# A planned scan kernel: the plan is told of the eight DMA semaphores, and dt and dt u are stored by chunks

## The chip, the core and the metric

The kernel runs on one core of a Trainium2 chip. The core has engines that each work through their own list of instructions in order: PE (TensorE, matmuls), DVE (VectorE), ACT (ScalarE), POOL (GpSimd) and SP (SyncE). SP computes nothing here; it issues transfers between the chip's memory and the core's on-chip memory. ACT and POOL issue some transfers too. The metric is the device time of one execution in microseconds; less is better.

## What is computed

Two layers of a vision network on an input of 4 images with 384 channels of 32 x 32 points, all in f32. In each layer a state-space scan comes first and a feed-forward part after it:

```
x = x + conv0(ln_c(x));  t = tokens(x);  t = t + ffn0(ln_t(t));  x = from_tokens(t)
x = x + conv1(ln_c(x));  t = tokens(x);  t = t + moe1(ln_t(t));  x = from_tokens(t)
```

`conv0` scans each image in four directions (rows, columns and both backwards), `conv1` is a Mamba block with 768 inner channels. The heart of both is the same recurrence over the 1024 points, with 16 states for each channel:

```
def step(h, inp):
    dtt, ut, bt, ct = inp
    dA = jnp.exp(dtt[..., None] * A)
    h = h * dA + (dtt * ut)[..., None] * bt[:, :, None, :]
    y = jnp.einsum('bkdn,bkn->bkd', h, ct)
    return (h, y)
```

dt, B and C come from projections of the input (`x_proj`, `dt_proj`, with a softplus on dt). `moe1` sends each token to the two best of four experts (384 to 1536 to 384 channels) and adds their outputs by gate weights.

## The kernel before

**The scan.** It is cut into 48 passes. A pass is one half of an image (T = 512 points) in one direction, or one half with half of the inner channels, for 384 channels. A pass has three parts (chunks of 128 channels), a part has four steps (four of the 16 states at a time): 576 steps in all. In a step the 128 partitions hold 32 channels times four states, and four groups x = 0..3 of 32 channels are treated one after the other:

- ACT computes the four decays exp(A dt) into PSUM tiles `da` (L1784) from the tile `dts`.
- POOL computes dt u times B for all four groups into a tile `s` (L1778) from `dtus` and `bt`; there are four `s` tiles.
- DVE runs the four recurrences (L1793) and multiplies some of the results by C (L1842); POOL multiplies the others (L1858). How many of the four POOL takes is chosen step by step by the plan (`split`). In a first half, the last column is kept in `state` (L1808 on DVE, L1857 on POOL).
- PE sums over the states into `acc` (L1814), and DVE adds `acc` to the output after the fourth step (L666 to L672, L918).

**What a pass needs first.** Two passes form a quad, which shares one projection: SP loads its weights `wx` (and `dtw`) from `ask_quad0` (L651, L652), PE multiplies (L637), ACT copies the result to `xd` (L642) and issues the store of the B and C rows (L494). `prep_pass` makes dt and dt u (L529 to L568) in tiles of [128 partitions, 3 chunks, 512], and `spread_out` (L511 to L514) stores both to a tile `spread` in the chip's memory, laid out as [chunk, 32 channels, group, 512]. `spread_pass` then reads it part by part, each row going to four partitions (the four states): on SP's queue one load of 1 MB into one of two `dtus` tiles (L590), on ACT's queue two loads of 512 KB into the three half tiles `dts` (L596). A `dtus` tile comes free when POOL has done the part before the last; the second `dts` half of a part has about one step between the decay that frees its tile and the decay that needs it. The rows of B and C are loaded for each pass by SP into `bt` and `ct` (L1775).

**Beside the scan** run layer norms, the feed-forward part of layer 0 (`post0`), the input projections and convolutions of layer 1 (`prep1`), its output (`post1`) and the experts (weights `mw` loaded at L1355, matmuls L1420 and L1442). What is left of the experts after the last scan forms the tail.

**What sets the order.** A planner in the kernel's Python (`Plan`) writes the order of each engine's list by simulating them before the kernel is built. An operation has a cost, the keys that it waits for, and so a time at which it could start; `run` takes the one that starts first, by the rules in `choose`, and emits it. Side work is written as generators: `yield SP, land(192)` asks for SP and says when the transfer will have landed. `land(kb)` is 3.5 + kb/200 us; an issue keeps SP for 0.1 us in the plan, whatever it issues. Where the plan sees PE idle, `fill` emits small matmuls that keep PE busy (L1833). The plan fixes the order alone; on the chip the instructions wait for semaphores.

**The semaphores of transfers.** In the built program every transfer that SP or ACT issues adds to one of eight semaphores, taken in turn over both queues, and waits, before it is issued, until the earlier transfer on that semaphore has landed, the eighth before it (2268 of the 2432 transfers carry this wait; others wait for a later one). An issue of ACT's that waits holds up ACT's other work. The plan before knows nothing of this.

Of the kernel before, what the change touches and what calls it, by code (L numbers as in the profile page):

```python
# [133 lines left out]

class Lane:
# [18 lines left out]
    def ready(self):  # L154
        return max(self.want[2] if len(self.want) > 2 else self.end, self.floor) + SLACK[self.rank >= LOW][self.want[0]]
# [11 lines left out]
class Plan:  # L167
# [39 lines left out]
    def mains(self, e):  # L207

        out = []
        for k in range(len(self.streams.get(e, ()))):  # L210
            op = self.head(e, k)
            if op is not None and all(d in self.end for d in op.deps):
                t = max([self.end[d] + LAG for d in op.deps], default=0.0) + op.lag
                out.append((max(self.free[e], t), k, op))
        return out
# [18 lines left out]
    def run(self):  # L234
        while True:
# [22 lines left out]
            start, what, e = best  # L258
            self.stuck = max(self.stuck, start)
# [4 lines left out]
            if isinstance(what, Lane):  # L264
# [5 lines left out]
                what.go(what.end, start)  # L270
            else:
# [4 lines left out]
                op.emit()  # L276


@with_exitstack
def layers(ctx, tc, ins, out, const):  # L280
# [160 lines left out]

    def layernorm(src, dst, eps, sq=None, sq_at=0.0, centred=False, scaled=True):
# [41 lines left out]
    def wload(src):  # L484

        w = yield from wts.take()
        yield SP, land(192) + 2.5
        nc.sync.dma_start(out=w.rearrange("p c m -> p (c m)"), in_=src)
        return w

    def rows_out(q, to):

        q["rows"] = q.get("rows") or dram.tile([2 * NS, L], F32, tag="rows", name="rows", bufs=4)
        nc.scalar.dma_start(out=q["rows"][:, to], in_=xd[q["at"] : q["at"] + 2 * NS, to])  # L494
# [12 lines left out]
    def load_dtw(q, k):  # L507

        nc.sync.dma_start(out=dtw[dt_rows(q), :], in_=ins["w_dt1"][:, k * D : (k + 1) * D])

    def spread_out(to, of):  # L511

        for q in range(NG):
            nc.sync.dma_start(out=to[:, :, q, :].rearrange("c r t -> r c t"), in_=of[q * QP : (q + 1) * QP])  # L514
# [60 lines left out]
    def spread_pass(p):  # L575
# [3 lines left out]
        def gen():  # L579
            spread, stored = st.pop(("spread", p))  # L580
            for part in range(NC):
# [8 lines left out]
                nc.sync.dma_start(out=dtus[n % 2].rearrange("p q t -> p (q t)"), in_=of(1, 0, NG))  # L590
                plan.end["dtu", p, part] = plan.now + land(1024)
                for x in range(2):
                    m = 2 * n + x - 3
                    before = (yield from until(("da", 4 * (m // 2) + 3, 2 * (m % 2) + 1))) if m >= 0 else 0.0
                    yield ACT, 0.55, max(before, stored)
                    nc.scalar.dma_start(out=dts[(2 * n + x) % 3].rearrange("p q t -> p (q t)"), in_=of(0, 2 * x, 2))  # L596
# [5 lines left out]
    def prep0(b):  # L602
        u = st[("u0", b)]

        def ln(h):
            def gen():
                yield SP, land(768)
                nc.sync.dma_start(out=u[h], in_=half(x_in[b], h))
                yield from layernorm(u[h], u[h], eps6)
# [38 lines left out]
    def ask_quad0(q, k):  # L648
        def gen():
            yield SP, land(66)  # L650
            nc.sync.dma_start(out=wx0.rearrange("p c m -> p (c m)"), in_=ins["w_x0"][k])  # L651
            nc.sync.dma_start(out=dtw[dt_rows(q), :], in_=ins["w_dt0"][k])  # L652
# [21 lines left out]
    def post0(b, h):  # L674
# [15 lines left out]
        def add_x(c):  # L690
            def gen():
                xh = yield from t1.take()
                yield SP, land(256)
                nc.sync.dma_start(out=xh, in_=piece(x_in[b], c, h))
# [8 lines left out]
        def ln2():  # L703
# [8 lines left out]
            nc.sync.dma_start(out=fold[:, :, :32], in_=fold_d)  # L712
# [14 lines left out]
        def ffn(lane):  # L727
            def gen():
# [6 lines left out]
                for i in range(2 * lane, 2 * lane + 2):  # L735
                    w, proj1 = yield from wts.two()
                    yield SP, land(192) + 2.0
                    nc.sync.dma_start(
                        out=w.rearrange("p a m -> p (a m)")[zrow, :], in_=ins["w_fc1"][:, i * NC * P : (i + 1) * NC * P]
                    )  # L740
                    nc.sync.dma_start(
# [29 lines left out]
        def ffn_out():  # L771
# [4 lines left out]
            nc.sync.dma_start(out=spread.rearrange("p a m -> p (a m)"), in_=of)  # L776
# [12 lines left out]
            nc.sync.dma_start(out=half(x1[b], h), in_=y)  # L789
# [11 lines left out]
    def prep1(b, h):  # L801
# [6 lines left out]
        def conv(i):  # L808
            def gen():
                for j in range(NC):  # L810
# [8 lines left out]
                    nc.sync.dma_start(out=dg, in_=taps_d[c])  # L819
# [33 lines left out]
        def gate(i):  # L853
            def gen():
# [14 lines left out]
                nc.scalar.dma_start(out=to.rearrange("(c p) t -> p c t", p=P), in_=z)  # L869
# [16 lines left out]
    def prep_quad1(q, b, h):  # L886
        def gen():
# [3 lines left out]
            nc.sync.dma_start(out=wx1, in_=ins["w_x1"].rearrange("p (c m) -> p c m", c=NI))  # L891
# [28 lines left out]
    def post1(b, h, early=False):  # L920
# [3 lines left out]
        def gate(i):  # L924
            def gen():
# [3 lines left out]
                nc.sync.dma_start(out=z, in_=of.rearrange("(c p) t -> p c t", p=P))  # L929
# [14 lines left out]
        def project():  # L944
            o = st["o", b, h] = yield from tmp.take()
            for m in range(NC):
                w = yield from wts.two()
                yield SP, land(384)
                for i in range(2):
                    nc.sync.dma_start(out=w[i], in_=w_out[m, :, i * NC : (i + 1) * NC])  # L950
# [20 lines left out]
        def add_x(m):  # L971
            def gen():
# [3 lines left out]
                nc.sync.dma_start(out=xh, in_=piece(x1[b], m, h))  # L976
# [12 lines left out]
        def end():  # L989
            o = st["o", b, h]  # L990
            t = yield SP, STORE
            nc.sync.dma_start(out=x2[b, h].rearrange("(c p) t -> p c t", p=P), in_=o)
# [16 lines left out]
    def centre():  # L1009
# [9 lines left out]
        for c in range(NI):  # L1019
# [7 lines left out]
            nc.sync.dma_start(out=taps_d[c], in_=dg)  # L1027
            t1.give(dg)
        plan.end["taps",] = plan.now
        for i in range(2):  # L1030
# [4 lines left out]
            nc.sync.dma_start(out=w, in_=ins["w_out"][i * D : (i + 1) * D].rearrange("(c p) m -> p c m", p=P))  # L1035
# [8 lines left out]
            for m in range(NC):  # L1044
                nc.sync.dma_start(out=out_d[m, :, i * NC : (i + 1) * NC], in_=w[:, :, m * P : (m + 1) * P])
            tmp.give(t)

    def zero():
# [4 lines left out]
        for slot in (*slot_x, *slot_y):  # L1053
            for x in range(slot.shape[0] // P // n):
                to = slot.rearrange("(n p) d -> p n d", p=P)[:, n * x : n * (x + 1), :]
                yield SP, 12.0
                nc.sync.dma_start(out=to, in_=rep(z[:, :D], n))
# [265 lines left out]
    def experts():  # L1323
# [21 lines left out]
        def weights():  # L1345

            for s, i in every:
# [4 lines left out]
                for q in range(2 * NQ):  # L1352
                    w = yield from mws.take()
                    yield SP, 0.1
                    nc.sync.dma_start(out=w, in_=of[q])  # L1355
                    wq.append((plan.now + land(393) + 1.0, w))

        def fetch():

            for n, (s, i) in enumerate(every):  # L1360
# [11 lines left out]
                nc.sync.dma_start(  # L1372
# [3 lines left out]
                nc.sync.dma_start(  # L1376
# [115 lines left out]
        def keep():  # L1492

            for s0, _ in every:
# [16 lines left out]
                for k in range(m):  # L1511
                    yield SP, land(192)
                    nc.sync.dma_start(out=slot_y[g % 3][bass.DynSlice(at + k * P, P)], in_=rows[k][:, :D])
# [6 lines left out]
    def combine(u):  # L1520
# [4 lines left out]
        def begin():  # L1525
            x = st["out", u] = yield from tmp.take()
            yield SP, land(768)
            nc.sync.dma_start(out=x, in_=x2[u].rearrange("(c p) t -> p c t", p=P))

        def some(j):  # L1530
            def gen():
# [10 lines left out]
                nc.sync.dma_start(out=b2, in_=ins["b2"])  # L1542
# [30 lines left out]
        def end():  # L1573
# [3 lines left out]
            nc.sync.dma_start(out=to, in_=x)  # L1577
# [3 lines left out]
        def early():  # L1581
# [3 lines left out]
            nc.sync.dma_start(out=b2[:NE, :D], in_=ins["b2"])  # L1585
# [9 lines left out]
        def by_rows(j):  # L1595
            def gen():
# [32 lines left out]
                nc.sync.dma_start(out=to, in_=part)  # L1629
# [143 lines left out]
    def load(p, m, of, to):  # L1773
        rows = passes[p]["q"]["rows"][of + 4 * m : of + 4 * m + 4, cols(passes[p]["h"])]
        nc.sync.dma_start(out=to[m], in_=rows.unsqueeze(0).to_broadcast([QP, 4, T]))  # L1775
# [211 lines left out]

    plan = Plan(
# [10 lines left out]
def land(kb):  # L1999

    return 3.5 + kb / 200
# [105 lines left out]
```

## Time and profile before

| what | value |
|---|---|
| three runs | 5034.54, 5049.6, 5051.74 us (median 5049.6) |
| profiled execution | 5032.81 us, its span 5031.0 us, mean granted clock of PE 0.894 |
| busy over the span | PE 85%, DVE 83%, POOL 80%, ACT 60% |
| first and last scan of DVE | 99.4 us and 4472.7 us |
| transfers | 899.33 MB, 179 GB/s |

The page's second part shows the span in 40 slices (tenths of each engine's time):

```profile
PE   8777778887767799988877798899888888899999
DVE  4999999999999899999989999999999999850002
ACT  4544458765545577767654577767685756554442
POOL 2999999999988898989988988889899988850002
```

DVE and POOL are at nine tenths until the scan ends, some 35 slices in; PE takes over for the tail. The transfers of interest, from the page's last part (what, queue, count, size of one):

```profile
dts<-dts ACTq DMA_DIRECT2D x288, 512.0 KB
dtus<-dts SPq DMA_DIRECT2D x144, 1024.0 KB
dts<-tmp SPq DMA_DIRECT2D x376, 192.0 KB
```

The name `dts` stands for the half tiles, and also for the `spread` tile in the chip's memory: `dts<-dts` is a load from the one to the other, and `dts<-tmp` is a store of `spread_out` (eight more read from another pool, 384 in all). The time of a landing is not on the page; where one is given, it is the last update of the transfer's semaphore in the trace.

### The profile page before, as it was taken

What the parts mean: (1) busy time and instruction counts of PE and PEld (TensorE: products, weight loads), DVE (VectorE), ACT (ScalarE), POOL (GpSimd) and SP (SyncE); (2) the same over time, 40 slices, a digit from 0 to 9 for tenths busy, and PEclk for the clock granted to TensorE, in tenths of its full rate; (3) what the DMA queues carried; (4) which work ended last, traced back from release to release, by engine and by line L of the source; (5) the groups of instructions that cost most, each with busy time, mean ns of one, the idle gap of its engine ahead of it and who ended that gap; (6) DMA issues with size and microseconds to landing.
All of it is one profiled execution on the core that took longest, in us unless ns stands there. A gap on an engine that the chain in (4) does not pass through costs nothing. (4 is left out here: it accounts for less than half of the span.)

```text
span 5031.0 us, 57132 instructions
## 1 busy us (share of the span) xinstructions
PE 4262.9 (85%) x17967; PEld 2192.9 (44%) x17967; DVE 4159.0 (83%) x5754; ACT 3037.3 (60%) x4769; POOL 4006.4 (80%) x1826
## 2 busy tenths in 40 slices
PE   8777778887767799988877798899888888899999
PEld 3222222222223454444444454345534333569996
DVE  4999999999999899999989999999999999850002
ACT  4544458765545577767654577767685756554442
POOL 2999999999988898989988988889899988850002
PEclk9887889888888899999987899899988889899998
DMA  4344656654443565556564655466655454655556
GB/s 148 110 161 156 205 169 214 207 185 139 161 143 107 195 193 175 190 188 211 188 221 161 215 181 175 155 197 205 230 179 191 155 181 148 220 184 180 170 165 190
DMA packets 394191, 899.33 MB, mean 179 GB/s; under 512 B 62384, under 2 KB 143520, under 8 KB 375456
## 3 DMA queue, kind: packets, MB, share of 16 engines
q1 hardware_dynamic: 336672, 704.28, 43.3%
q10 hardware_dynamic: 49024, 166.22, 9.7%
q0 software_dynamic: 8192, 25.17, 1.6%
q8 instruction: 143, 2.34, 0.2%
q14 instruction: 160, 1.31, 0.1%
HBM read 712.11 MB, written 183.40 MB: 178 GB/s over the span
## 5 line engine op out<-in xcount | busy, mean ns | idle before, releaser
L1778 POOL TENSOR_TENSOR s<-dtus,bt 128x2048 f32<-128x2048 f32 x576 | 2605.3, 4533 | 178.1 <-PE acc L1814 67.2
L1784 ACT ACTIVATE da<-dts,a 128x512 f32<-128x512 f32 x2304 | 1530.2, 686 | 886.4 <-DVE s L1842 771.5
L1814 PE MATMUL acc<-s,four 128*32 128x512 f32 x4608 | 735.1, 682 | 382.0 <-POOL s L1858 344.9
L1858 POOL TENSOR_TENSOR s<-s,ct 128x512 f32<-128x512 f32 (+1 forms) x552 | 942.5, 1708 | 138.6 <-DVE s L1793 102.0
L1793 DVE TENSOR_TENSOR_SCAN da<-da,s 128x512 f32<-128x512 f32 x775 | 918.2, 1216 | 114.0 <-ACT da L1784 82.4
L1842 DVE TENSOR_TENSOR s<-da,ct 128x512 f32<-128x512 f32 x1529 | 1009.6, 680 | 0.1
L1793 DVE TENSOR_TENSOR_SCAN da<-da,state,s 128x512 f32<-128x512 f32 x754 | 939.5, 1277 | 17.7 <-ACT da L1784 10.1
L1833 PE MATMUL acc<-ident,few 128*32 128x256 f32 x2886 | 751.5, 416 | 36.2 <-DVE big L918 18.6
L1833 PEld LDWEIGHTS acc<-ident,few 128*32 128x32 f32 x2886 | 334.4, 119 | 510.6 <-issue 225.1
L1793 DVE TENSOR_TENSOR_SCAN s<-da,state,s 128x512 f32<-128x512 f32 x398 | 495.5, 1267 | 8.7 <-ACT da L1784 8.6
L1793 DVE TENSOR_TENSOR_SCAN s<-da,s 128x512 f32<-128x512 f32 x377 | 447.1, 1204 | 17.3 <-ACT da L1784 17.3
L1814 PEld LDWEIGHTS acc<-s,four 128*32 128x32 f32 x4608 | 106.5, 113 | 748.9 <-POOL s L1858 547.3
L1420 PE MATMUL ps<-tmp,mw 128*128 128x256 f32 (+1 forms) x1812 | 387.9, 369 | 22.3 <-ACT tmp L1465 11.5
L1442 PE MATMUL ps<-mw,tmp 128*128 128x192 f32 x2096 | 377.1, 337 | 17.5 <-DMA mw<-in_w_dram 6.8
L1442 PEld LDWEIGHTS ps<-mw,tmp 128*128 128x128 f32 x2096 | 350.4, 195 | 82.4 <-issue 42.9
L1420 PEld LDWEIGHTS ps<-tmp,mw 128*128 128x128 f32 x1812 | 316.5, 198 | 135.7 <-issue 30.4
L1615 DVE SCALAR_TENSOR_TENSOR big<-big,gk,da 128x384 f32<-128x384 f32 x2 | 1.2, 612 | 414.2 <-PE da L1613 414.2
L1605 POOL DMA_INDIRECT big<-ys,slot x12 | 11.8, 980 | 382.7 <-DMA ys<-t 379.3
L799 PE MATMUL ps<-big,w 128*128 128x512 f32 x576 | 280.2, 627 | 14.3 <-DMA w<-in_w_in_dram 8.2
L568 POOL TENSOR_TENSOR tmp<-tmp,big 128x256 f32<-128x256 f32 (+1 forms) x186 | 193.0, 1063 | 68.3 <-DVE tmp L1037 68.3
L529 PE MATMUL ps<-xd,dtw 12*128 12x512 f32 (+1 forms) x288 | 187.9, 743 | 17.2 <-ACT tmp L542 9.4
L838 PE MATMUL ps<-tmp,t 128*128 128x512 f32 x368 | 175.3, 620 | 15.6 <-ACT tmp L830 9.9
(448 smaller groups left out, 5322.2 us busy)
## 6 DMA issues: line engine op xcount, KB each, us to landing
mw<-in_w_dram SPq DMA_DIRECT2D x414, 384.0 KB
dts<-dts ACTq DMA_DIRECT2D x288, 512.0 KB
dtus<-dts SPq DMA_DIRECT2D x144, 1024.0 KB
dts<-tmp SPq DMA_DIRECT2D x376, 192.0 KB
bt<-rows SPq DMA_DIRECT2D x192, 256.0 KB
ct<-rows SPq DMA_DIRECT2D x192, 256.0 KB
dts<-in_w_dram SPq DMA_DIRECT2D x78, 384.0 KB
ys<-t SPq DMA_DIRECT2D x32, 768.0 KB
```

The lines of the kernel that those rows point to most:

```text
L529: nc.tensor.matmul(pd, lhsT=dtw[dt_rows(q), c * P : (c + 1) * P], rhs=xd[dt_rows(q), cols(h)], start=True, stop=True,)
L568: nc.gpsimd.tensor_tensor(to, by, u[:, c], ALU.mult)
L799: nc.tensor.matmul(pi, lhsT=w[:, c, :], rhs=u[:, c], start=c == 0, stop=c == NC - 1)
L1420: nc.tensor.matmul(ph[:, k * width : (k + 1) * width], lhsT=w[:, c, k * P : (k + 1) * P], rhs=turned[:, c], start=c == 0, stop=c == NC - 1,)
L1442: nc.tensor.matmul(py[:, k * HD : (k + 1) * HD], lhsT=by_f(hids[half_], width)[:, at_, k * P : (k + 1) * P], rhs=w[:, f], start=4 * q + f ...
L1778: nc.gpsimd.tensor_tensor(ss[i % NSR], dtus[part_of(i) % 2], rep(bts[i % 4], NG), ALU.mult)
L1784: nc.scalar.activation(das[x], dts[(2 * part_of(i) + x // 2) % 3][:, x % 2, :], AF.Exp, scale=v["a"][:, g, m : m + 1])
L1793: nc.vector.tensor_tensor_scan(d if in_psum else s, d, s, 0.0 if v["first"] else state[:, v["slot"], j, x : x + 1], ALU.mult, ALU.add)
L1814: nc.tensor.matmul(acc[x * QP : (x + 1) * QP, :], lhsT=four, rhs=ss[i % NSR][:, x, :], start=m == 0, stop=m == 3)
L1833: nc.tensor.matmul(acc[:QP, : 2 * P], lhsT=nil.to_broadcast([P, QP]), rhs=rep(ident, 2), start=fresh, stop=fresh)
L1842: nc.vector.tensor_tensor(ss[i % NSR][:, x, :], das[x], cts[i % 4], ALU.mult)
L1858: nc.gpsimd.tensor_tensor(s[:, m:, :], s[:, m:, :], rep(cts[i % 4], NG - m), ALU.mult)
```

## The change

It has two parts. First, the planner keeps a model of the eight semaphores (`Ring`): every transfer of SP and ACT goes through `ask`, which notes when the transfer could be issued, keeps the queue for 0.55 us, and computes a landing from a common rate of 220 KB/us. No transfer is planned before the eighth before it has landed by this model. `land` is changed with it. The times of tiles that are given back follow from these.

Second, `spread_out` stores one chunk per transfer (three of 256 KB, each from all 128 partitions) in place of one group of 32 channels per transfer (four of 192 KB, each from 32 partitions). What is stored, and where, is the same.

```diff
+class Ring:
+    at = busy = 0.0
+    lands = [0.0] * 8
+    n = 0
...
+    @classmethod
+    def next(cls):
+        return cls.lands[cls.n % 8] + 0.1
+
+    @classmethod
+    def issue(cls, kb):
+        t = max(cls.at, cls.next())
+        cls.busy = max(t + 1.2, cls.busy) + kb / RATE
+        cls.lands[cls.n % 8] = cls.busy + 1.0
+        cls.n += 1
+        cls.at = t + ISSUE
...
     def ready(self):
-        return max(self.want[2] if len(self.want) > 2 else self.end, self.floor) + SLACK[self.rank >= LOW][self.want[0]]
+        least = Ring.next() - LAG if self.want[0] == SP or len(self.want) > 3 else 0.0
+        return max(self.want[2] if len(self.want) > 2 else self.end, self.floor, least) + SLACK[self.rank >= LOW][self.want[0]]
...
                 t = max([self.end[d] + LAG for d in op.deps], default=0.0) + op.lag
-                out.append((max(self.free[e], t), k, op))
+                out.append((max(self.free[e], t, Ring.next() if e == SP else 0.0), k, op))
...
             start, what, e = best
+            Ring.at = start
...
                 what.go(what.end, start)
+                self.free[e] = max(self.free[e], Ring.at) if Ring.at > start else self.free[e]
...
                 op.emit()
+                if e == SP:
+                    self.free[e] = max(self.free[e], Ring.at)
...
+    def ask(queue, out, in_):
+        Ring.issue(int(np.prod(out.shape)) / 256)
+        queue.dma_start(out=out, in_=in_)
...
     def spread_out(to, of):
-        for q in range(NG):
-            nc.sync.dma_start(out=to[:, :, q, :].rearrange("c r t -> r c t"), in_=of[q * QP : (q + 1) * QP])
+        for c in range(NC):
+            ask(nc.sync, out=to[c].rearrange("r q t -> q r t"), in_=of[:, c])
...
-                    yield ACT, 0.55, max(before, stored)
-                    nc.scalar.dma_start(out=dts[(2 * n + x) % 3].rearrange("p q t -> p (q t)"), in_=of(0, 2 * x, 2))
+                    yield ACT, 0.55, max(before, stored), True
+                    ask(nc.scalar, out=dts[(2 * n + x) % 3].rearrange("p q t -> p (q t)"), in_=of(0, 2 * x, 2))
...
+    Ring.reset()
     plan = Plan(
...
 def land(kb):
-    return 3.5 + kb / 200
+    return 3.2 + kb / 220
+
+RATE, ISSUE = 220.0, 0.55
```

All other issues of SP and ACT inside the planned part are changed from `dma_start` to `ask` in the same way. Since the plan's times move, the whole order moves with them: the built program has 2336 transfers of SP and ACT instead of 2432, DVE's multiplications by C are 1514 instead of 1529, and the filling matmuls (L1833) are 1538 instead of 1443.

## The prediction

> **What bounds the kernel now.** I read the windows view first, cut at the first scan (99 us) and the last one (4474 us).
>
> ```profile
> core 0: us, PE busy (x) PEld busy (x) DVE busy (x) ACT busy (x) POOL busy (x), PEclk, DMA share, GB/s
> 99.00:4474.00 4375.00, 3624.02 (x14791) 1688.88 (x14791) 4082.64 (x5459) 2766.88 (x4312) 3949.51 (x1769) 0.88 0.54 179
> 4474.00:5031.00 557.00, 548.89 (x2891) 467.29 (x2889) 43.43 (x127) 224.26 (x381) 46.75 (x45) 0.96 0.58 178
> ```
>
> For 4375 us DVE is busy 93% and POOL 90%: the scan phase, 576 steps of 7.6 us, ends when DVE has done its work and its 292 us of idle time. After it PE is busy 99% with the experts that are left. In the built order of instructions the matmuls after the last scan sum (L1814) are the same in both kernels, 688 of L1442 and 540 of L1420 among them, so I cost the tail at nothing (at most its 8 us of idle PE could go); its weight loads would cost something only if they came later than now. All of the change must show in the scan phase.
>
> There I ask which of DVE's waits a transfer ends, in the view of all waits (total us, times, longest):
>
> ```profile
> ACT xd L642 <- PE ps L637: 106.8, 14, 15.7
> PE ps L637 <- DMA wx<-in_w_x_dram: 93.8, 12, 14.9
> DVE da L1793 <- ACT da L1784: 92.5, 39, 14.1
> POOL s L1778 <- DMA dtus<-dts: 39.8, 4, 19.9
> ACT da L1784 <- DMA dts<-dts: 35.0, 14, 6.5
> ```
>
> Read downwards the first three are one chain: the weights of a quad (wx) land late, PE's L637 waits, the copy L642 waits in ACT's queue, the decays L1784 wait behind that copy, and DVE runs dry. I followed each DVE gap over 1.5 us back through its releasers. Seven gaps end in this chain (4.8, 9.9, 5.9, 7.9, 14.1, 7.3 and 5.0: 55 us); four end in late dts or dtus loads (19 us); three in the store L789 (12 us). So 86 of DVE's 292 idle us are owed to transfers. The other gaps (among them 94 us behind PE's sums) have nothing to do with them.
>
> Why wx is late shows in SP's timeline at one such place (columns: start, length, what):
>
> ```profile
> 1657.84 3.68 SPq L514 DMA_DIRECT2D dts<-tmp  x4
> 1662.24 0.54 SPq L1775 DMA_DIRECT2D bt<-rows  x1
> 1662.89 0.58 SPq L1775 DMA_DIRECT2D ct<-rows  x1
> 1663.53 0.59 SPq L590 DMA_DIRECT2D dtus<-dts  x1
> 1664.21 8.83 SPq L514 DMA_DIRECT2D dts<-tmp  x4
> 1673.09 0.43 SPq L651 DMA_DIRECT2D wx<-in_w_x_dram  x1
> ```
>
> wx stands right behind the four stores of dt u. Those took 8.83 us to issue, because each waits for the transfer eight before it. PE waits for wx until 1675.4, ACT copies at 1680.9, and DVE's 14.1 us gap ends at 1683.6.
>
> **The change, part by part.**
>
> *The work.* By the built order, DVE's multiplications by C (L1842) go from 1529 to 1514 and its state copies (L1808) from 775 to 762: 15 x 0.680 + 13 x 0.147 = 12.1 us less. POOL takes them: 6 more double ones (2.355 us each), 3 more single (1.270), 5 more copies (0.19): 18.9 us. Cover for that: POOL's 425 idle us in the phase; without it, +18.9. Term: -12.
>
> *Stores by chunk.* 384 stores of 192 KB become 288 of 256 KB; bytes and 2 KB pieces stay the same. What moves is the outermost dimension of the DRAM side: 32 rows before, four groups of 32 channels now. The trace has one transfer with a four outermost, the load of spread_d (L776, 8 times, 192 KB). In the record of semaphore updates it shows five, the first after 1.0 us and four that come with the data; a store of the kernel before shows sixteen. It lands after 4.8 to 13.1 us, median 5.7; a 192 KB load over sixteen lands after 2.4 us when the queues are quiet. So a four outermost means four of the sixteen DMA engines. In that row the four stands on the source's side, in the new stores on the destination's. [...] If a four on the destination's side did nothing, the stores would run on sixteen as now, and the terms for wx and for the other transfers would fall to nothing: -22 in place of +73. I take four, as the row has it.
>
> A store is then 32 pieces on each of four engines; a 2,048-byte packet took 105 ns in the mean: 3.4 us, and 10.1 us for three stores. With the 2.5 us that a quiet spread load takes beyond its own 32 packets (4.8 less 32 x 0.071), the last lands 12.6 us after the first issue. The 96 groups of four in the trace had their last landing 6.1 us after the first issue (median). Difference: 6.5 us later. Readers of the stores don't notice: in both orders 44 of 48 passes store five to ten steps (38 us and more) before their first load. What is queued behind the stores notices.
>
> *wx, behind them.* In the new order wx still stands right behind a dt u store at 13 of 16 quads, so it comes 6.5 us later: 85 us over all. The new schedule answers with ACT's copy L642, which moves by one step later in all over those quads (five moves of 0.5 to 2.75 steps later, three of 0.75 to 3.25 earlier, the rest a quarter or none): 7.6 us of relief. Of PE's lateness DVE saw all at the seven quads that already stall (45 us) and, I take it, half at the other six (20). Term: +55. Bounds: -55 (the stalls vanish) and +85.
>
> *The other transfers.* Each pass (91 us) puts 192 pieces, 20.2 us, on each of the four engines, where it put 5.0 on each of sixteen. Of the 144 dts loads that have only a step to land in, 22% meet a store under way: 32. Each has 8 packets of 191 ns on an engine, 1.5 us, and sharing doubles it; fourteen already come late and the rest has hardly more room. Term: +25, bounds 0 and +109 (32 times one whole store, 3.4 us). ACT's own issues wait for the transfer eight before too; where that is a store (47 issues, as before) nine instead of seven come within a step of it. The decays are queued behind such an issue, and DVE waits for those. Term: +10, bounds 0 and 9 x 6.5 = 59. The dtus and bt loads follow the stores in SP's queue, but have four steps to land in: +5, bounds 0 and 40 (POOL's waits for dtus once over).
>
> *The schedule that knows.* Each issue now costs 0.55 us in the plan instead of 0.1, and none goes before the transfer eight back has landed. An issue took 0.33 to 0.59 us in the trace, so this is nearer the truth. But the plan lands a 256 KB store 3.4 us after its issue, and by the row above that is too early by 2 to 7 us. It can remove what is left of DVE's waits for transfers, 31 us; I take a third. Term: -10, bounds -31 and +25 (a reshuffled order with new small gaps). POOL's and PE's queues are reordered with it; no row prices that beyond this bound.
>
> Sum: -12 + 55 + 25 + 10 + 5 - 10 = +73 us. The profiled execution took 5032.8 us for its span of 5031.0, below all three runs (5034.5, 5049.6, 5051.7). The middle of the four is 5042, so I predict **5115 us**.
>
> **The rivals.**
>
> *The knowledge pays.* If stores that land 6.5 us later are hidden (eight steps of room), and the plan puts PE's L637 and ACT's copies where wx really lands, about half of the 86 us goes with the 12: 5042 - 55 = 4987; all of it, 4944. For it: the chain is caused by just what the plan did not know. Against it: wx still stands behind the same stores, at the same steps. It decides from the point where ACT's waits for L642 fall below some 50 us. Chance of faster: 0.22.
>
> *It does not do what it says.* The order around the quads hardly moves, and what the plan gains the stores give back: 5042 - 12 + 10 = 5040, within 5017 to 5067. Chance 0.14.
>
> *The ring closes.* The eight semaphores are held by slow stores, and ACT itself is held at its issues: half of 47 x 6.5 us on top of the sum gives 5270. Against it: at only nine of the 47 does the store stand close. Chance 0.05, part of the slower side.
>
> *The forecast*, slower: 0.59, its own range 5070 to 5185. A measurement of this kernel can tell 0.5%, 25 us, from no change. Faster by more than that 0.22, within 0.14, slower 0.64. The range reaches down into the first rival and up past the middle of the bounds: 4985 to 5185.
>
> **What would show it.** Stores L514 with five semaphore updates instead of sixteen and a last landing 12 us after the first issue: the engine count. "ACT xd L642 <- PE ps L637" growing from 107 to 150 us or more: the wx term; falling below 60: the first rival. "ACT da L1784 <- DMA dts<-dts" above 60: the shared engines. The last scan at about 4545 us and a tail of 557: that the tail stays out of it. Sixteen updates on the new stores would make the prediction wrong at its root.

## The result and the profile after

| | before | after |
|---|---|---|
| runs | 5034.54 to 5051.74 us, median 5049.6 (5) | 5199.88 to 5216.13 us, median 5207.18 (5) |
| profiled span | 5031.0 us | 5209.6 us, granted clock of PE 0.887 |
| start of DVE's first scan, end of its last | 99.4 and 4474 us | 103.7 and 4648 us |

The change makes the kernel 3.3% slower: ratio 1.033, 95% interval 1.0315 to 1.0344. In the medians that is 158 us, in the two profiled spans 179 us. The prediction said slower, and 5115 us; the time lies above its range.

The windows view of after, cut at the first and the last scan, answers to the one shown of before (columns: busy us and count of each engine, granted clock, DMA share, GB/s):

```profile
104.00:4648.00 4544.00, 3669.46 (x14971) 1721.77 (x14972) 4070.59 (x5431) 2765.03 (x4312) 3967.03 (x1783) 0.88 0.51 173
4648.00:5209.60 561.60, 552.94 (x2906) 469.53 (x2904) 43.43 (x126) 224.31 (x381) 46.32 (x45) 0.96 0.58 177
```

Of the 179 us, 169 lie in the scan phase (4544 against 4375). DVE's work there fell, by 12.0 us (4082.6 to 4070.6); its idle time rose from 292 to 473 us. The tail is 5 us longer (561.6 against 557.0), the start 4 us.

The waits view of after (total us, times, longest) shows the chain from before grown at every link:

```profile
DVE da L1829 <- ACT da L1820: 220.4, 78, 16.6
ACT xd L678 <- PE ps L673: 190.9, 14, 20.7
...
PE ps L673 <- DMA wx<-in_w_x_dram: 153.6, 12, 19.3
...
ACT da L1820 <- DMA dts<-dts: 35.2, 14, 6.2
...
POOL s L1814 <- DMA dtus<-dts: 26.4, 1, 26.4
ACT da L1820 <- DMA dts<-tmp: 26.4, 4, 8.8
```

(L1829, L1820, L678 and L673 are L1793, L1784, L642 and L637 of before; all issues are now at L476, in `ask`.) PE waits 154 us for wx instead of 94, ACT's copy 191 instead of 107, DVE 220 instead of 93. The waits for dts and dtus loads, on which another term of the prediction stood, have not grown. The last line is new. (An "..." in a fence marks lines that are not shown.)

One place in the timeline of after shows the whole chain (start, length, engine, what, idle time before and its releaser):

```profile
1317.24 2.11 SPq L476 DMA_DIRECT2D dts<-tmp  x3
1319.40 3.22 SPq L476 DMA_DIRECT2D dtus<-dts  x1
1322.66 1.09 SPq L476 DMA_DIRECT2D wx<-in_w_x_dram  x1
...
1334.07 5.35 PE L673 MATMUL ps<-big,wx 128*44 128x512 f32 x12 [15.94 <-DMA wx<-in_w_x_dram]
...
1339.47 0.58 ACT L678 COPY xd<-ps 44x512 f32<-44x512 f32 x1 [20.69 <-PE ps L673]
1339.95 0.69 ACT L1820 ACTIVATE da<-dts,a 128x512 f32<-128x512 f32 x1
...
1340.74 1.29 DVE L1829 TENSOR_TENSOR_SCAN da<-da,state,s 128x512 f32<-128x512 f32 x1 [16.25 <-ACT da L1820]
```

Three stores of dt u go out from 1317.2 on; wx is issued at 1322.7, and PE starts only at 1334.1, 11.4 us after that issue. ACT's copy follows, the decays stand behind it in ACT's queue, and DVE has been idle for 16 us when its scan starts at 1340.7.

How late the transfers land was read from the updates of their semaphores (medians; a landing is the last update, counted from the issue):

| transfer | before | after |
|---|---|---|
| updates of one store `dts<-tmp` | 16 | 5 |
| its landing | 3.85 us | 11.16 us |
| a set of stores, first issue to last landing | 6.1 us (four) | 15.1 us (three) |
| wx, behind the stores of dt u | 2.80 us | 11.19 us |
| ct loads, median and 90th percentile | 4.12, 7.0 us | 5.44, 11.4 us |
| w_in loads, the same | 3.74, 6.2 us | 4.34, 9.9 us |
| dts loads (ACT's queue) | 5.87 us | 6.16 us |

A new store shows its five updates at 0.95, 10.01, 10.04, 10.08 and 12.05 us (one store as an example): the first at once, four with the data.

The packets tell the same. Between the first issue and the last landing of a set of stores, 23 sets of before and three of after have no 2 KB packets on SP's queue but their own 384. In before 16 of them are in flight at once most often (31% of that time, never more than 20), in after four (62%, never more than six).

The updates of wx show what those stores do to it. Its load counts sixteen. In before the 12th comes after 2.60 us and the 16th after 2.80 (medians of 16 loads). In after the 12th comes after 3.39 us, and the last four follow late: the 16th after 11.19. At the 14 loads that are issued while stores are under way, the step of over 1 us between the 12th update and the 13th is there every time, and at 13 of the 14 the last update comes 0.2 to 0.3 us after the last of those stores has landed. So twelve parts of the load are as good as on time, and four, as many as the parts of a store, end when the stores do.

To size the terms, every gap of DVE over 0.2 us between the first and the last scan was followed back through its releasers to the transfer, or to the engine where the trail ends (us of DVE's idle time; smaller groups, 80 us before and 89 us after, are only in the last row):

| gap ends in | before | after |
|---|---|---|
| wx | 72 | 167 |
| a store (`dts<-tmp`) that has not landed | 0 | 34 |
| other loads on SP's queue: w_in, mw, expert rows `tmp<-xs`, fold, taps, ct | 31 | 70 |
| dts loads | 13 | 6 |
| dtus loads | 14 | 0 |
| the store L789 (`x<-big`) | 12 | 4 |
| ACT's decays, no transfer found | 57 | 90 |
| all | 279 | 460 |

### The profile page after: what moved, and what is told of

The parts are those of the page before. It is cut to its first block, busy times and chain, and to the rows that moved or that the text cites. A ratio compares the mean times of both kernels' runs of the same rounds, so it can differ in the third digit from the quotient of the medians.

```text
span 5209.6 us, 57475 instructions
## 1 busy us (share of the span) xinstructions
PE 4311.9 (83%) x18157; PEld 2227.7 (43%) x18157; DVE 4147.1 (80%) x5726; ACT 3035.6 (58%) x4769; POOL 4024.1 (77%) x1840
## 3 DMA queue, kind: packets, MB, share of 16 engines
q1 hardware_dynamic: 331680, 704.26, 40.8%
## 5 line engine op out<-in xcount | busy, mean ns | idle before, releaser
L1820 ACT ACTIVATE da<-dts,a 128x512 f32<-128x512 f32 x2304 | 1529.9, 686 | 854.0 <-DVE s L1878 692.2
L1894 POOL TENSOR_TENSOR s<-s,ct 128x512 f32<-128x512 f32 (+1 forms) x561 | 960.4, 1713 | 149.9 <-DVE s L1829 114.8
L1829 DVE TENSOR_TENSOR_SCAN da<-da,s 128x512 f32<-128x512 f32 x762 | 902.9, 1216 | 175.3 <-ACT da L1820 142.3
L1829 DVE TENSOR_TENSOR_SCAN da<-da,state,s 128x512 f32<-128x512 f32 x752 | 936.4, 1276 | 80.0 <-ACT da L1820 78.1
L1869 PE MATMUL acc<-ident,few 128*32 128x256 f32 x3076 | 784.1, 410 | 35.1 <-DVE big L954 13.9
L1869 PEld LDWEIGHTS acc<-ident,few 128*32 128x32 f32 x3076 | 352.4, 118 | 526.3 <-issue 227.8
L1829 DVE TENSOR_TENSOR_SCAN s<-da,state,s 128x512 f32<-128x512 f32 x400 | 498.0, 1266 | 30.2 <-ACT da L1820 30.2
L1829 DVE TENSOR_TENSOR_SCAN s<-da,s 128x512 f32<-128x512 f32 x390 | 462.4, 1205 | 24.3 <-ACT da L1820 24.1
L1456 PE MATMUL ps<-tmp,mw 128*128 128x256 f32 (+1 forms) x1752 | 366.2, 365 | 22.3 <-DMA mw<-in_w_dram 14.2
L1456 PEld LDWEIGHTS ps<-tmp,mw 128*128 128x128 f32 x1752 | 303.6, 197 | 123.7 <-issue 46.7
```

Of the source, the lines that this page charges most:

```text
L1456: nc.tensor.matmul(ph[:, k * width : (k + 1) * width], lhsT=w[:, c, k * P : (k + 1) * P], rhs=turned[:, c], start=c == 0, stop=c == NC - 1,)
L1820: nc.scalar.activation(das[x], dts[(2 * part_of(i) + x // 2) % 3][:, x % 2, :], AF.Exp, scale=v["a"][:, g, m : m + 1])
L1829: nc.vector.tensor_tensor_scan(d if in_psum else s, d, s, 0.0 if v["first"] else state[:, v["slot"], j, x : x + 1], ALU.mult, ALU.add)
L1869: nc.tensor.matmul(acc[:QP, : 2 * P], lhsT=nil.to_broadcast([P, QP]), rhs=rep(ident, 2), start=fresh, stop=fresh)
L1894: nc.gpsimd.tensor_tensor(s[:, m:, :], s[:, m:, :], rep(cts[i % 4], NG - m), ALU.mult)
```

## The experiments

A ratio is to the runs of before that went with the kernel on the same chip. Those medians were 5038 to 5068 us, so ratios are compared and not times. The traces show what may be part of the difference: late in the tail of `chunks_only`, `know_groups`, `dtu_chunks`, `know_true`, `chunks_act`, `land_only` and the two `know_groups_wx` runs, PE stands still for 24 to 25 us in all at the transposes of the result (L1621, L1657 of after), whichever kernel it is; before, after and the other runs do not have this, though `chunks_only` has the order of before. What it comes from is not known. It lies behind the last scan, so a comparison of scan phases does not contain it.

**The two halves of the change, apart.** `chunks_only` is before with the chunk stores; planner and order are untouched.

```diff
     def spread_out(to, of):
-        for q in range(NG):
-            nc.sync.dma_start(out=to[:, :, q, :].rearrange("c r t -> r c t"), in_=of[q * QP : (q + 1) * QP])
+        for c in range(NC):
+            nc.sync.dma_start(out=to[c].rearrange("r q t -> q r t"), in_=of[:, c])
```

> The kernel before with the stores of dt and dt u by chunks alone (three of 256 KB in place of four of 192 KB); the plan and so the order of all other instructions are those of before. Theory E (the four DMA engines of a chunk store are the whole loss): 5170 to 5230 us, ratio 1.024 to 1.036, the stores show five semaphore updates and land 10 us or more after their issue, wx 8 us or more later than before. Theory P (the new plan is most of the loss, a store's lateness is hidden): within 5030 to 5080. Theory S (my forecast's own sum, wx alone): about 5110.

`know_groups` is after with the four group stores of before, through `ask` (that edit the other way round).

> The changed kernel with the stores as before (four of 192 KB, one for each group of 32 channels) but planned with the eight semaphores. Theory E: 4960 to 5050 us, since what the plan knows is left and the slow stores are gone; sixteen updates on the stores. Theory P: 5120 us or more. If knowledge neither pays nor costs: 5020 to 5060.

| | median us | ratio, 95% interval | DVE idle in its scan phase, us |
|---|---|---|---|
| chunks_only | 5288.05 | 1.0448 (1.043 to 1.0466) | 513 |
| know_groups | 5011.86 | 0.9903 (0.9887 to 0.992) | 291 |
| after | 5207.18 | 1.033 (1.0315 to 1.0344) | 473 |

The halves pull in opposite directions and nearly add up: +4.5% and -1.0% make +3.5%, where after has +3.3%. The parts do not add up in the same way: with group stores the new plan leaves DVE's idle time as it was (291 us against 292), with chunk stores it takes 40 us off it (473 against 513). The stores alone lose more than the whole change does. In `chunks_only` the order is that of before, so no order can be blamed. Its waits view:

```profile
DVE da L1793 <- ACT da L1784: 209.4, 61, 21.6
ACT xd L642 <- PE ps L637: 186.2, 16, 24.1
...
PE ps L637 <- DMA wx<-in_w_x_dram: 174.5, 12, 21.8
...
ACT da L1784 <- DMA dts<-dts: 60.4, 28, 7.1
PE ps L1386 <- DMA tmp<-xs: 59.9, 12, 10.8
```

It is the picture of after: PE's wait for wx 94 to 175 us, and behind it the loads of expert rows (`tmp<-xs`), 22 to 60 us. Each store shows five updates and lands after 10.4 us, wx after 10.7. In `know_groups` a store shows sixteen and lands after 3.71 us, wx after 3.56, and the same lines are at or below those of before:

```profile
DVE da L1829 <- ACT da L1820: 92.0, 47, 12.6
...
ACT xd L678 <- PE ps L673: 89.9, 12, 15.4
...
PE ps L673 <- DMA wx<-in_w_x_dram: 52.5, 8, 12.3
```

**Only dt u by chunks.** `dtu_chunks` is before with chunk stores for dt u alone, the set that wx stands right behind.

```diff
...
-        spread_out(spread[1], dtu)
+        spread_out(spread[1], dtu, True)
```

(With the new argument `spread_out` stores by chunks, as above, and without it by groups.)

> The kernel before with dt u alone stored by chunks, dt by groups; plan of before. wx stands right behind the dt u stores. If the loss is wx waiting behind the dt u stores in SP's queue (theory W), most of it is here already: 5120 to 5180 us. If it is the load on the four engines and the semaphores that the stores hold (theory L), about half of the loss of both: 5090 to 5130. Theory P: as before, 5030 to 5070.

5181.87 us, ratio 1.0231 (1.0214 to 1.0248): half of the loss of `chunks_only` for half of its stores. The DVE gaps that end in wx are 134 us (72 in before, 154 in `chunks_only`), so this half holds three quarters of the wx term; of the gaps that end in the other loads and in stores, the dt set brings most. So it is neither wx alone nor an even share of one load on the engines.

**A plan that is told the price.** `know_true` is after with the chunk stores planned at three times their bytes, so that the plan lands a set of three some 7 us later than it did (3.5 us for each store in place of 1.2).

```diff
-            ask(nc.sync, out=to[c].rearrange("r q t -> q r t"), in_=of[:, c])
+            ask(nc.sync, out=to[c].rearrange("r q t -> q r t"), in_=of[:, c], times=3)
```

(`ask` multiplies the bytes that it tells `Ring` by `times`.)

> The changed kernel, with a chunk store planned at three times its bytes (3.5 us each in a row, as 32 pieces of 105 ns on one engine give, in place of 1.2). The plan then knows when such stores land. If the loss comes from a plan that believes in fast stores: well below the changed kernel, 5080 to 5150 us. If the four engines cost the same whatever the plan believes: 5180 to 5220.

5385.62 us, ratio 1.0632 (1.0614 to 1.065): the slowest of all, and outside both ranges expected. The wx gaps did fall, from 167 to 74 us, but others took their place:

```profile
DVE s L1878 <- DMA ct<-rows: 95.2, 7, 37.9
...
PE ps L673 <- DMA wx<-in_w_x_dram: 91.1, 9, 14.5
ACT da L1820 <- DMA dts<-dts: 90.8, 29, 7.9
```

DVE itself now waits for ct, up to 38 us at once. `Ring` has one `busy` for all transfers, so a store that is planned longer pushes back every transfer after it, also those that use other engines. I take that to be why loads were put off until they were late; no run tests it.

**The engine count, by itself.** `chunks16` is `chunks_only` with the DRAM side written over 128 rows first. Same stores, same bytes, same 2 KB pieces, same order. It leaves out the order of the channels that the loads rely on, so it measures time alone. Its pieces also follow each other in memory, where those of `chunks_only` lie 8 KB apart; but those of the group stores lie 8 KB apart too, and land after 3.85 us with sixteen updates.

```diff
-            nc.sync.dma_start(out=to[c].rearrange("r q t -> q r t"), in_=of[:, c])
+            nc.sync.dma_start(out=to[c].rearrange("r q t -> (r q) t"), in_=of[:, c])
```

> The plan and the order of before, with three chunk stores of 256 KB whose DRAM side runs over 128 rows first (same bytes, same three stores as chunks_only, same 2 KB pieces); channels come to lie at other places of the chunk than the loads expect, so what is computed differs from the reference. Theory E (what costs is that a store whose slowest dimension is 4 is dealt to four engines, not that there are chunks): each store counts 16 updates and lands in about 4 us (chunks_only: 5 updates, 10.4 us), wx<-in_w_x_dram in 3 to 5 us, DVE's idle time between first and last scan near before's 290 us (chunks_only 513), time 5010 to 5075 us. Rival S (three stores of 256 KB are slow because of their size, pieces or place in the queue, whatever the number of engines): landing 8 us or more, time 5200 to 5290 us.

`know_chunks16` makes the same edit in the changed kernel.

> The changed kernel with the same 128-row chunk stores; what is computed differs from the reference in the same way. Theory E: landing about 4 us, 16 updates, time near know_groups (5012 us): 4980 to 5030 us. Rival S: as after, 5180 to 5210 us. If E holds for chunks16 and this one stays above 5050 us, plan and chunks disagree in something besides the landing.

| | updates, landing of a store | wx lands after | median us | ratio, 95% interval |
|---|---|---|---|---|
| chunks_only | 5, 10.40 us | 10.67 us | 5288.05 | 1.0448 (1.043 to 1.0466) |
| chunks16 | 16, 4.97 us | 4.26 us | 4990.18 | 0.9903 (0.9887 to 0.992) |
| after | 5, 11.16 us | 11.19 us | 5207.18 | 1.033 (1.0315 to 1.0344) |
| know_chunks16 | 16, 4.75 us | 3.77 us | 4966.3 | 0.9863 (0.9846 to 0.9879) |

The pages count the packets of SP's queue (packets, MB, share), in this order for before, `chunks_only` and `chunks16`:

```profile
q1 hardware_dynamic: 336672, 704.28, 43.3%
q1 hardware_dynamic: 331680, 704.26, 39.5%
q1 hardware_dynamic: 335136, 704.28, 41.5%
```

The bytes are all but the same. The differences to before, 4992 and 1536, are those of the 4-byte packets in the traces, and they are 384 x 16 less 288 x 4 and 384 x 16 less 288 x 16: one such packet for each update that comes with the data. That, the packets in flight and the four late updates of wx are what "four engines" rests on.

This isolates the cause. What costs is neither a chunk nor 256 KB nor three stores in place of four, but the outermost four. Dealt over sixteen engines, chunk stores do not merely cost nothing, they gain 1.0% in the plan of before, a little more than I expected, and 0.4% in the new one (0.9863 against 0.9903 of `know_groups`). Why they beat the groups is not settled: a set lands 7.4 us after its first issue, later than the four groups (6.1), and wx does not land earlier either (8.5 us after the first store's issue, median, against 7.0). No run has chunk stores over sixteen engines with their pieces 8 KB apart. The wait lines of `chunks16` show only where the time came from:

```profile
DVE da L1793 <- ACT da L1784: 99.9, 42, 15.8
...
ACT xd L642 <- PE ps L637: 82.2, 14, 14.0
...
PE ps L637 <- DMA wx<-in_w_x_dram: 52.2, 7, 12.0
```

**Behind in the queue, or sharing the engines?** A load issued on SP after a four-engine store could be late because it stands behind it in SP's queue, or because four engines are busy, whoever asks. `chunks_wx_act` is `chunks_only` with the loads of `ask_quad0` on ACT's queue; `groups_wx_act` is the same edit in before, as a control. (The edit also changes the plan's order, in both alike.)

```diff
-            yield SP, land(66)
-            nc.sync.dma_start(out=wx0.rearrange("p c m -> p (c m)"), in_=ins["w_x0"][k])
-            nc.sync.dma_start(out=dtw[dt_rows(q), :], in_=ins["w_dt0"][k])
+            yield ACT, 0.9
+            nc.scalar.dma_start(out=wx0.rearrange("p c m -> p (c m)"), in_=ins["w_x0"][k])
+            nc.scalar.dma_start(out=dtw[dt_rows(q), :], in_=ins["w_dt0"][k])
```

> chunks_only, with the two loads of ask_quad0 (wx<-in_w_x_dram and its dtw) issued from ACT's queue and not from SP's behind the chunk stores. Theory Q (the loads wait because they stand behind the stores in SP's queue, on the same rings): wx lands in 3 to 5 us (chunks_only 10.7), PE's wait for it goes from about 150 us back to about 70, time 5288 less 80 to 100 = 5190 to 5215 us. Theory F (the loads wait at the four engines themselves, whichever queue they come from): wx lands in 8 us or more, time 5260 to 5310 us.

> Control for chunks_wx_act: before with the same two loads on ACT's queue. Both theories: the loads land in about 3 us as in before, ACT pays two issues of about 0.5 us a pass; time 5020 to 5080 us. Whatever it differs from before by is to be taken off chunks_wx_act's gain.

`chunks_act` is `chunks_only` with the stores, and nothing else, on ACT's queue.

```diff
-            nc.sync.dma_start(out=to[c].rearrange("r q t -> q r t"), in_=of[:, c])
+            nc.scalar.dma_start(out=to[c].rearrange("r q t -> q r t"), in_=of[:, c])
```

> chunks_only (5288 us, ratio 1.045) with the chunk stores issued from ACT's queue, so that none of SP's loads stands behind them; the plan does not know it. Theory Q (loads are late because they stand behind a four-engine store in one queue): the stores themselves still take 10 us, but on SP's queue the median and the 90th percentile go back to those of before (wx 3 to 4 us, tmp<-xs 90th percentile under 7, ct under 7.5); the dts loads, which now stand behind the stores, get later; six more issues a pass on ACT cost up to 288 x 0.56 = 160 us of ACT's time, part of it in front of its exponentials; ratio 1.005 to 1.035. Theory F (the loads wait at the four engines whichever queue they come from): SP's landings stay as in chunks_only, ratio 1.04 or more.

| | wx lands after | `tmp<-xs`, 90th percentile | dts loads, 90th percentile | ratio, 95% interval |
|---|---|---|---|---|
| before | 2.80 us | 6.3 us | 8.2 us | 1 |
| chunks_only | 10.67 | 10.2 | 8.3 | 1.0448 (1.043 to 1.0466) |
| chunks_wx_act | 5.35 | 10.2 | 8.4 | 1.0276 (1.0255 to 1.0297) |
| groups_wx_act | 2.91 | 6.6 | 8.3 | 0.999 (0.998 to 0.9999) |
| chunks_act | 5.88 | 8.8 | 12.9 | 1.0332 (1.0315 to 1.035) |

Mostly the queue, and partly the engines. Of the 7.9 us by which wx is late in `chunks_only`, 5.3 go when it is issued from the other queue; 2.4 remain against the control, more than expected of a pure queue. The control is not quite alike: only 4 of its 16 loads are issued while stores are under way, against 13 in `chunks_wx_act`. The updates of wx show both parts without it:

| | 12th update of wx | 16th update |
|---|---|---|
| before | 2.60 us | 2.80 us |
| chunks_only | 3.43 | 10.67 |
| chunks_wx_act | 3.20 | 5.35 |
| chunks_act | 3.53 | 5.88 |
| chunks16 | 3.48 | 4.26 |

In the same queue the last four updates wait until the stores have landed (0.2 us later at 12 of 14 loads of `chunks_only`). From the other queue they are still some 2 us late, but in `chunks_wx_act` wx lands before the last store at 9 of the 13 loads with stores under way, by up to 6 us.

In `chunks_act` the picture turns over: on SP's queue wx comes back to 5.88 us (3 to 4 were expected, a miss for the pure queue) and the expert rows halfway (ct too: 8.2 us at the 90th percentile, 11.8 in `chunks_only`, under 7.5 expected), while the dts loads, which now stand behind the stores in ACT's queue, go from 8.2 to 12.9 us at the 90th percentile. The waits follow the stores to the new queue (view of all waits, `chunks_act`):

```profile
DVE da L1793 <- ACT da L1784: 256.8, 89, 11.2
...
ACT da L1784 <- DMA dts<-dts: 97.6, 25, 9.3
ACT da L1784 <- DMA dts<-tmp: 82.6, 23, 12.6
...
PE ps L637 <- DMA wx<-in_w_x_dram: 44.0, 7, 8.8
```

PE's wait for wx is down to 44 us and ACT waits 180 us in its place, so of the 4.5% only 1.2 are gained back. What a load gains from the other queue depends on the stores it leaves behind: nothing with stores that show sixteen updates (`groups_wx_act`: wx 2.91 us against 2.80, ratio 0.999), while with these its landing halves (10.67 to 5.35 us in `chunks_wx_act`), and 1.7% of the time goes with it.

**What the knowledge is worth, and where.** `land_only` is before with the new estimate of a landing and no `Ring`.

```diff
-    return 3.5 + kb / 200
+    return 3.2 + kb / 220
```

> Before, with the new estimate of a landing alone (3.2 + kb/220 instead of 3.5 + kb/200); no shared semaphores, no time of an issue, group stores. If the gain of know_groups (ratio 0.990) comes from the estimate: ratio 0.988 to 0.993. If it comes from the eight semaphores and the time of an issue: 0.997 to 1.003.

5102.36 us, ratio 1.0065 (1.004 to 1.0091). The gain of `know_groups` is not the estimate; alone, that loses a little, which no theory had expected. So it lies in the semaphores, the time of an issue, or the estimate together with them, and in the order that comes out. Its DVE is idle as long as in before (291 against 292 us); the profile's 25 us are 19.3 us less work in the scan phase (4063.3 against 4082.6) and a first scan 5 us earlier. The medians differ by twice that. Most of the rest lies in the tail:

```profile
94.50:4448.50 4354.00, 3680.49 (x15202) 1738.53 (x15200) 4063.30 (x5434) 2771.48 (x4322) 3970.16 (x1784) 0.90 0.54 181
4448.50:5005.60 557.10, 527.68 (x2769) 446.60 (x2768) 43.33 (x127) 217.26 (x368) 45.45 (x45) 0.94 0.54 173
```

It is as long as the 557.0 us of before, but PE has 21 us less to do in it (527.7 against 548.9): more of the experts was done before the last scan. What hides this in the two spans is the stall of 25 us at L1657, which this trace has and that of before has not.

**Better than both.** The plan, before and after, counts the quad's weights as there at their issue, so PE is always sent to wait. In `know_groups_wx` the plan waits for the landing ("Theory W" below is this one's own).

```diff
-            yield SP, land(66)
+            t = yield SP, land(66)
             ask(nc.sync, out=wx0.rearrange("p c m -> p (c m)"), in_=ins["w_x0"][k])
             ask(nc.sync, out=dtw[dt_rows(q), :], in_=ins["w_dt0"][k])
+            yield from till(lambda: plan.now >= t)
```

> The changed kernel with the four 192 KB group stores of before (as know_groups, 5012 us, ratio 0.990), and a plan that does not call the quad's weights there before wx<-in_w_x_dram has landed by its estimate (until now the load's job is done at its issue, so PE's first multiplication with wx is planned at the issue and always waits). Theory W (that wait is a fault of the plan that other work can fill): PE's wait for wx falls from about 60 us to under 20 us, ratio to before 0.980 to 0.987. Rival: the work behind wx is late whichever way it is planned, ratio 0.988 to 0.995.

5017.65 us, ratio 0.9901 (0.9884 to 0.9918). PE's wait for wx falls from 52.5 to 29.8 us, short of the 20 us hoped for, and the time does not move. That does not refute the theory for the scan phase, which is 19 us shorter (4334.8 us against 4354.0), although the gaps that end in PE's sums rose by 38 us (40.8 to 78.9). The tail takes it back: it is 28 us longer (585.2 against 557.1), since PE has 26 us more of its work left in it (553.7 against 527.7).

`know_groups_wx_act` is `know_groups` with the two loads on ACT's queue (the edit of `groups_wx_act`, through `ask`).

> know_groups with the two loads of ask_quad0 on ACT's queue. As groups_wx_act differs from before by a ratio of 0.999 only: ratio 0.987 to 0.992; if standing behind the group stores costs the newer plan more than the old one, 0.980 to 0.986.

4991.54 us, ratio 0.9849 (0.9833 to 0.9866): faster than before, after and `know_groups`, whose intervals it does not touch. The wx gaps fall from 40 to 25 us, those behind the expert rows from 28 to 2, those of ct from 14 to 1. Its scan phase is 40 us shorter (4313.9 us), of which the tail (585.0 us) takes back 28. It is the version to keep. `know_chunks16` ends at the same ratio within the intervals, but needs the channels in another order; that a chunk store over sixteen engines can be had together with the right order was not shown.

## Why the prediction was right in sign and short in size

**Four engines.** Right, and the root of it all: five updates as foreseen, `chunks16` shows that the loss goes with the four, and four of wx's updates show where it strikes. With the four on the destination's side a store shows the five updates that the one row of before shows with a four on the source's (L776), and mostly four packets in flight where the stores of before have sixteen.

**The landing.** Mis-sized. I put the last landing of a set 12.6 us after the first issue, 6.5 us later than the 6.1 of before; measured 15.1, 9.0 later. The estimate added packet times and a quiet load's overhead and was 2.5 us too short; what took the rest, no run shows.

**wx.** The term of the sum that was mis-sized most: "+55. Bounds: -55 (the stalls vanish) and +85." DVE's gaps that end in wx grew by 95 us, past the bound. At 13 quads 9.0 us later is 117; the full lateness reached DVE at most of them, not half of it at six, and ACT's copy, moved by a step over all, brought little relief. The number of gaps went from 9 to 13.

**The other transfers.** The step whose mechanism failed: "Of the 144 dts loads that have only a step to land in, 22% meet a store under way", +25 us for sharing engines, estimated to double the 1.5 us of a load's packets, which no run shows. The dts gaps fell from 13 to 6 us and their landing moved from 5.87 to 6.16 us. They are on ACT's queue. What was late were loads on SP's queue behind the stores, which I had costed for dtus and bt alone (+5; dtus and its 14 us went to zero). Not costed at all, and without a reason given, were the side loads: w_in, mw, the expert rows, fold, taps, ct, whose gaps grew by 39 us. Most of their readers are multiplications in PE's list and copies in ACT's, with the scan's work queued behind them. I had asked "what is queued behind the stores" and then followed wx only.

**Stores that hold something.** ACT's issues behind the transfer eight before were put at +10, up to 59. DVE's gaps that end in a store are 34 us, part of them this term and part one that I missed. This place in the timeline of after shows the first kind:

```profile
3010.24 6.83 SPq L476 DMA_DIRECT2D dts<-tmp  x3
...
3015.59 0.52 ACTq L476 DMA_DIRECT2D dts<-dts  x1
3016.15 1.91 ACT L1820 ACTIVATE da<-dts,a 128x512 f32<-128x512 f32 x3 [8.78 <-DMA dts<-tmp]
```

ACT stood 8.8 us at the issue of a dts load until a store had landed. The second kind is a tile that comes free late: `ACT tmp L493 <- DMA dts<-tmp` (13.7 us) is ACT about to write a tile that a store still reads. "Readers of the stores don't notice" was right, but the tiles' next writers do.

**The work.** -12, measured 12.0 less in the scan phase. **The tail** at nothing: 5 us.

**The knowledge.** -10 of a possible -31, for fewer waits of DVE. By the ratio of `know_groups` the gain with group stores is 1.0%, 49 us, and it is not that: DVE's idle time stays, and the traces show 19 us less work on DVE, a start 5 us earlier and 21 us less for PE in the tail. The rival that rested on the knowledge named a true gain, by luck rather than by its reason; it lost because the stores take four times as much.

The measured parts add up to -12 (work), +181 (gaps), +4 (start) and +5 (tail) = 178, against 178.6 in the spans, as they must. That is 105 us over the sum of 73: wx is 40 of it, the side loads 39, the stores that hold something 24; the dts loads are 32 below their term and dtus with bt 19 below theirs. A part that no term stood for: 33 us of the gaps end in ACT's decays without a transfer behind them; what they stem from stays open.

## What to carry to other kernels

Before a transfer's shape is changed, look at the outermost dimension of both sides and at the number of semaphore updates that a like transfer shows: here fewer, longer stores with an outermost four took 11.2 us to land in place of 3.9. Price a slow transfer by everything that stands behind it in its queue, by the tiles that it keeps, and by the issues that wait for its semaphore; its own reader may be the only one that does not notice. Try the parts of a change apart: here a gain of 1.0% was hidden under a loss of 4.5%.

## What the hardware showed that I had not expected

A load that counts sixteen updates was held back 7.9 us by stores that show four with their data when both came from SP (wx, 10.67 us against 2.80), and 2.4 us when the queues differed (5.35 us against 2.91). Twelve of its updates had come after 3.4 us and only the last four waited, in the same queue until the stores ahead of it had landed (0.2 us later at 12 of 14 loads). The traces do not name the engine of an update, so that the four are the engines of the stores is read from the counts and the times.

And telling the plan more is no sure gain: three edits that touch only what it is told moved the time by -1.0% (`know_groups`), +0.65% (`land_only`) and, by the price of a store alone, from +3.3% to +6.3% (`know_true`).
